# A two-layer graph attention kernel: the step whose sums are split into pieces runs for nearly all superchunks, with another order inside

## The chip, the cores and the metric

The kernel runs on one core of a Trainium2 chip. The metric is the device time of one execution in microseconds (us). The kernel before was timed three times: 4126.3, 4113.4 and 4116.05 us, median 4116.05. Besides, one execution was recorded by the hardware profiler; all durations below come from that one.

## The reference: what is computed

A graph has 6250 nodes with 256 features and 200000 directed edges with 32 features each, sorted by target node. After a layer norm and a relu, two graph attention layers follow, the first with 4 heads, the second with 1. Cut to what matters:

```python
te = relu(edge_attr @ We + be) * exp(x @ Wo + bo)[src][:, None]      # edge features
hx = (x @ Wg).reshape(n, h, f)
al = leaky_relu((hx . a_s)[src] + (hx . a_d)[dst] + ((te @ Wge) . a_e), 0.2)   # logits
m  = segment_max(al, dst);  al = exp(al - m[dst])
al = al / segment_sum(al, dst)[dst]
out = segment_sum(hx[src] * al[:, :, None], dst) + b
```

Each node also gets an edge to itself with the mean of its edges' features. The first layer's output plus its input goes through a relu into the second layer; the second layer's goes to the output. So every edge needs one row of a table indexed by its source (a gather), a softmax over all edges of one target, and a sum over all edges of one target.

## The kernel before: how the work is tiled and ordered

**Superchunks.** The edges lie in 1563 chunks of 128. A superchunk is 24 chunks; there are 66 per layer, the last two with 14 and 13 chunks. A superchunk (numbers 0 to 65 in layer 0, 66 to 131 in layer 1) takes one step of a loop (L611 to L679). The program gives the order of the instructions of each engine by hand; each engine runs its own in that order and waits by semaphores for the others.

**The work of one superchunk,** by the names in the code:

- `gather` (L872): one indirect DMA per chunk on POOL (L881) brings 128 table rows into a buffer G. There are three such buffers, so the gather of superchunk k+1 overwrites that of k-2.
- `rphase1` (L956): the edge features. For each of two halves, TensorE products into the PSUM tile y (L965), then a Relu on ScalarE (L970, or L968 for odd sizes) into R. y and R exist once. `load_ea` loads the edge features of two superchunks on SyncE.
- `spread` (L982, in every second step for two superchunks), `parts` (L1012) and `blocks` (L1027): one-hot rows and the target's share of the logits; VectorE and one small product (L1024).
- `rphase2` (L974) and `adst` (L1035): products L979 and L1038 that put edge and target shares together in the PSUM tile zad; `edge_rows` (L1041) turns them on VectorE into rt (L1052) and sums them (L1055).
- `logits` (L1058): six small VectorE operations, the first of which (L1066) is the first to read the gathered rows; the last two are running maxima.
- `ends` (L1085, product L1089), `links` (L1091: two scans L1099 and L1101 on VectorE, product L1106) and `maxima` (L1108): the maximum over each target's edges, across partitions, then the exponentials on ScalarE (L1139).
- `scale` (L1167): one VectorE operation (L1174) multiplies all rows of G by their weights.
- `carried` (L1148): adds what the superchunk before has for a target that goes on into this one.
- `onehots` (L1002, L1009): the matrix S that maps edges to target nodes.
- `sums` (L1178): per chunk one product S^T G into the PSUM tile u (L1185; each is two records in the trace). It takes the chunks a to b, so it can be called in pieces.
- `evict` (L1187) and `carry` (L1192): ScalarE copies u to U; the row to be carried on is picked by a product (L1196) and copied (L1198).
- `finish` (L1305; in layer 0 L1246 to L1275): the node window's output, on VectorE with three ScalarE operations. `rows1` and `rows2` (layer 0): transposes (L1280) and the next layer's table rows (L385). `rows3`: adds the bias (L389) with an Exp (L1292) and writes the rows to layer 1's table (L1321); in layer 1 it writes the output.

**The normal step** of superchunk k (L630 to L677) issues, in this order: the gather and the edge features of k+1, logits, ends and links of k with all 24 chunks of the sums of k-1 in one block ahead of the link product, then one-hots of k, the finish of k-2, evict and carry of k-1, maxima and scaling of k, and edge rows of k+1.

**The step in pieces** (`tight`, L710, with `meet`, L695) serves the superchunks 62 to 64 of each layer (`tight = NS - 4` at L609). There, half of the sums of k run right behind its own scaling, and the rest in the next step, in two pieces on either side of `links`. The edge features of k+1 come late in it, behind the sums, the carry and the row products of k-2 (L735). Superchunk 64, whose next one is the last, has an order of its own (`final`), which finishes two node windows.

**The end of a layer** (`last`, L751). The first 24 gathers of layer 1 are issued ahead of the last step's work. They may read only table rows that are written: the indices of `redirect` (L806) leave out the last two node windows (64 and 65), whose share is added by products afterwards (`added`, L834). So that gather needs the table write of window 63, and the gather after it those of 64 and 65.

Of the kernel before, what the change touches and what calls it, by code (L numbers as in the profile page):

```python
# [32 lines left out]
C = 24  # L33
# [45 lines left out]
class Kernel:  # L79
# [311 lines left out]
    def indices(self, wp):  # L391
# [20 lines left out]
        self.base_f = base = cp.tile([P, NS], F32, name="base")  # L412
        V.tensor_copy(base, scf[:, 0, :])
        last, qbase, qlast = scf[:, 1, :], scf[:, 3:7, :], scf[:, 7:11, :]
        yield

# [41 lines left out]
        yield  # L458
        ll = wp.tile([P, NS], F32, name="ll", bufs=1)
        V.tensor_sub(ll, last, base)  # L460
        self.lsel = cp.tile([P, NS], F32, name="lsel")
        V.tensor_scalar(self.lsel, ll, self.iota_p, None, op0=OP.is_equal)
# [109 lines left out]
    def edges(self, ctx):  # L572
        nc = self.nc
        self.gp += [self.pool(f"gath{i}", 1, ctx) for i in range(1, 3)]
        self.sp = self.pool("onehot", 2, ctx)
        self.lp = self.pool("loads", 2, ctx)
        self.wp = self.pool("work", 2, ctx)
        self.np_ = self.pool("nodes", 2, ctx)
        self.xp = self.pool("index", 1, ctx)
        self.ps_y = self.pool("ps_y", 1, ctx, space=PSUM)  # L580
        self.ps_1 = self.pool("ps_1", 1, ctx, space=PSUM)
        self.ps_f = self.pool("ps_f", 1, ctx, space=PSUM)
        self.lf = self.ps_1.tile([P, 512], F32, name="lf")
        nc.vector.memset(self.lf[0:4, 0:1], -BIG)
        offs = np.concatenate([[0], np.cumsum(self.cs)]).tolist()
        steps = [dict(L=L, s=s, C=self.cs[s], o=offs[s], k=L.l * self.NS + s)
                 for L in self.L for s in range(self.NS)]
        self.state = {0: None, 1: None}
        self.early = self.cs[0] if self.NS > 1 else 0
        self.steps = steps  # L590
        self.nodes(steps[0])
        self.load_lb(0)
        self.load_ea(0)
        self.load_fl(0)
        self.gather(steps[0], self.CX)
        if self.NS % 2:
            self.load_lb(1)
        self.spread(steps[0])
        self.parts(steps[0])
        self.blocks(steps[0])  # L600
        drain(self.rphase1(steps[0]))
        self.load_ea(1)
        self.rphase2(steps[0])
        self.adst(steps[0])
        self.edge_rows(steps[0])

        pv = pf = pr = None

        tight = max(self.NS - 4, 1)  # L609
        self.ahead, self.rest = 1, None  # L610
        for k, st in enumerate(steps):  # L611
            nx = steps[k + 1] if k + 1 < len(steps) else None
            for q in steps[k + 1:k + 3]:
                if q["L"] is st["L"] and "tw" not in q:
                    self.nodes(q)
            self.load_lb(k + 2)
            left = self.groups[self.ahead][0] - 2 - k if self.ahead < len(self.groups) else 99
            if self.rest is None and left <= 2:
                gi = self.index_load(self.ahead, self.xp)
                self.rest = self.index_group(self.ahead, self.xp, gi)  # L620
            if st["s"] + 1 == self.NS:
                self.last(st, pv, nx)
                pv = pf = pr = None
                continue
            if st["s"] >= tight:
                self.tight(st, pv, pr, nx)
                self.index_on(left)
                pr, pv = pv, st
                continue
            self.gather(nx)  # L630
            drain(self.rphase1(nx))
            self.load_ea(k + 2)
            drain(self.logits(st))
            self.ends(st)
            self.spread(nx)
            self.parts(nx)
            if pv and "u" not in pv:
                self.sums(pv)
            self.links(st)
            self.load_fl(k + 1)  # L640
            self.blocks(nx)
            if k != self.NS:
                self.onehots(st)
            if pf:
                drain(self.finish(pf))
            if pv and "U" not in pv:
                self.evict(pv)
                self.carry(pv)
            if pf:
                self.rows1(pf)  # L650
            self.rphase2(nx)
            self.adst(nx)
            drain(self.maxima(st))
            if pf:
                self.rows2(pf)
            if k == self.NS:
                self.onehots(st)
            drain(self.scale(st))
            self.carried(st)
            enter = st["s"] + 1 == tight  # L660
            if enter:
                self.sums(st, 0, self.pieces(st)[0])
            elif st["s"] == 0:
                self.sums(st)
            if pf:
                self.rows3(pf)
            self.edge_rows(nx)
            if enter:
                self.onehots(nx)
                if pv:  # L670
                    drain(self.finish(pv))
                pr = pv
            elif st["s"] == 0:
                self.evict(st)
                self.carry(st)
            self.index_on(left)
            pf, pv = pv, st  # L677
            if k == 0 and self.early:
                self.redirect()  # L679
        self.flag()  # L680
# [9 lines left out]
    def pieces(self, st):  # L690

        c = st["C"]
        return (c + 1) // 2, c - c // 3

    def meet(self, st, pv, nx):  # L695

        p1, p2 = self.pieces(pv) if pv else (0, 0)
        drain(self.logits(st))
        self.ends(st)
        if nx:  # L700
            self.spread(nx)
            self.parts(nx)
        if pv:
            self.sums(pv, p1, p2)
        self.links(st)
        if pv:
            self.sums(pv, p2)
        self.load_fl(st["k"] + 1)

    def tight(self, st, pv, pr, nx):  # L710


        final = nx["s"] + 1 == self.NS
        self.gather(nx)
        self.meet(st, pv, nx)
        self.blocks(nx)
        if final:
            self.evict(pv)
            self.carry(pv)
            if pr:  # L720
                self.rows1(pr)
                self.rows2(pr)
                self.rows3(pr)
            drain(self.finish(pv))
            drain(self.maxima(st))
            self.rows1(pv)
            self.rows2(pv)
        else:
            drain(self.maxima(st))
            self.evict(pv)  # L730
            self.carry(pv)
            if pr:
                self.rows1(pr)
                self.rows2(pr)
        drain(self.rphase1(nx))  # L735
        self.load_ea(st["k"] + 2)
        self.rphase2(nx)
        self.adst(nx)
        if final:
            self.rows3(pv)  # L740
        drain(self.scale(st))
        self.carried(st)
        self.sums(st, 0, self.pieces(st)[0])
        if pr and not final:
            self.rows3(pr)
        self.edge_rows(nx)
        self.onehots(nx)
        if not final:
            drain(self.finish(pv))

    def last(self, st, pv, nx):  # L751
# [6 lines left out]
            nc.sync.dma_start(v[:, :early * P], self.srow.partition_broadcast(P))  # L758
        if not pv:
            self.onehots(st)  # L760
        self.meet(st, pv, None)
        if nx:
            nc.vector.tensor_scalar(self.src, self.src, 2.0, None, op0=OP.mult)
        drain(self.maxima(st))
# [687 lines left out]
def drain(g):  # L1452
    for _ in g:
        pass
# [93 lines left out]
```

## Time and profile before

| what | value |
|---|---|
| median of the runs | 4116.05 us |
| the profiled execution's own time | 4109.04 us |
| span of its instructions | 4107.1 us |
| busy: POOL, VectorE, TensorE, ScalarE | 2988.5, 2872.1, 2807.1, 545.5 us |
| gathers (L881) | 3114, mean 954 ns |
| sums (L1185) | 1700.2 us busy in 6252 records |
| scaling (L1174) | 853.2 us |
| clock granted to TensorE, mean | 0.789 |
| DMA moved | 584.74 MB, 142 GB/s |

The span runs from the first to the last instruction; the profiled execution's own time lies 1.9 us above it. A group's line in the profile gives the line of code, the engine, the operation, what is written and read, the count, then the total busy time in us, the mean of one in ns, and the engine's idle time just before them with what ended it. In a timeline each row is start, duration, engine, line, operation; an idle time before it stands in brackets with its releaser. "issue" is idle time for which the profile shows no releaser.

The order of the trace: the first gather in the loop's buffers starts at 89.62 us, layer 0's last at 2057.51 us, layer 1's first at 2097.34 us and its last at 4066.99 us.

### The profile page before, as it was taken

The page shows a single profiled execution, that of the slowest core. Times are in us where ns is not written, and L with a number is a line of the kernel's source. Part 1 is how long each engine was busy: PE and PEld are TensorE (multiplying, and loading weights), DVE is VectorE, ACT ScalarE, POOL GpSimd, SP SyncE. Part 2 cuts the span into 40 slices and gives each one's busy share as a digit, 9 for nine tenths or more (in the row PEclk, how much of TensorE's full clock was granted, in tenths as well). Part 3 has the DMA queues.
Part 4 walks back from the last instruction along what each step waited for, and adds up shares of the span by engine and source line. Part 5 has one row for each costly group of instructions (what it writes and reads, how often), then busy time and mean ns, then how long its engine had stood idle before and what let it go on. Part 6 is the DMA issues. An engine that isn't in the chain of part 4 may idle for free.

```text
span 4107.1 us, 34953 instructions
## 1 busy us (share of the span) xinstructions
PE 2807.1 (68%) x10144; PEld 1848.2 (45%) x10144; DVE 2872.1 (70%) x6571; ACT 545.5 (13%) x1256; POOL 2988.5 (73%) x3158
## 2 busy tenths in 40 slices
PE   7677677776777777777676666656666566665766
PEld 5344454444444444445444444434444344443444
DVE  8677777878778787787756666566665666656566
ACT  5111111111111111111111010010100101001001
POOL 2777777777777777777647777777777777777774
PEclk9778787787787887878887777877778777777778
DMA  6555554555555555555435455555445545555543
GB/s 213 157 149 143 155 149 137 154 149 138 151 149 145 146 151 151 139 155 148 122 99 151 131 144 142 136 139 145 134 137 145 142 132 143 142 137 137 145 132 82
DMA packets 246795, 584.74 MB, mean 142 GB/s; under 512 B 63162, under 2 KB 103640, under 8 KB 246530
## 3 DMA queue, kind: packets, MB, share of 16 engines
q0 software_dynamic: 150144, 422.82, 39.4%
q1 hardware_dynamic: 96035, 158.96, 12.3%
q8 instruction: 81, 1.33, 0.1%
q14 instruction: 119, 0.97, 0.1%
q10 hardware_dynamic: 416, 0.67, 0.1%
HBM read 547.98 MB, written 34.34 MB: 142 GB/s over the span
## 4 chain that ended last, share of the span: by engine, by line
POOL 38%; PE 24%; DVE 18%; issue 15%; DMA 2%; ACT 2%; DVEq 0%; SPq 0%; ACTq 0%; POOLq 0%
POOL G L881 38%; PE u L1185 19%; DVE G L1174 8%; PE y L965 2%; DMA G<-T,src 1%; DVE lb L994 1%; PE fin L1196 1%; DVE rt L1052 1%; ACT R L970 1%; PE fin L1280 1%; ACT carry L1198 1%; DVE G L1163 1%; DVE S L1009 0%; DVE t1row L389 0%; DVE G L1143 0%
## 5 line engine op out<-in xcount | busy, mean ns | idle before, releaser
L881 POOL DMA_INDIRECT G<-T,src x3114 | 2970.2, 954 | 1075.2 <-issue 995.8
L1185 PE MATMUL u<-G,S 128*128 128x270 f32 (+1 forms) x6252 | 1700.2, 438 | 26.3 <-DVE G L1174 26.3
L1185 PEld LDWEIGHTS u<-G,S 128*128 128x128 f32 x6252 | 1354.5, 219 | 370.6 <-issue 37.8
L1174 DVE TENSOR_TENSOR G<-G,kps 128x6144 f32<-128x6144 f32 (+2 forms) x140 | 853.2, 6099 | 0.0
L965 PE MATMUL y<-ea,webd 64*128 64x384 f32 (+1 forms) x1056 | 514.1, 617 | 447.1 <-ACT R L970 442.2
L965 PEld LDWEIGHTS y<-ea,webd 64*128 64x128 f32 x1056 | 215.3, 226 | 670.2 <-ACT R L970 523.1
L1009 DVE TENSOR_TENSOR S<-kps,loc 128x3072 f32<-128x3072 f32 x132 | 436.1, 3304 | 0.0
L1089 PE MATMUL lf<-ident,fb 128*36 128x128 f32 (+1 forms) x132 | 53.4, 404 | 531.6 <-DVE fb L1081 307.5
L1089 PEld LDWEIGHTS lf<-ident,fb 128*36 128x36 f32 (+1 forms) x132 | 15.7, 119 | 647.5 <-DVE fb L1081 365.9
L970 ACT ACTIVATE R<-y,webd 128x768 f32<-128x768 f32 x260 | 231.9, 892 | 555.4 <-PE y L965 555.3
L1120 DVE SCALAR_TENSOR_TENSOR m<-fpen,lf,m 128x24 f32<-128x24 bf16 (+1 forms) x66 | 16.6, 252 | 360.2 <-PE lf L1106 359.9
L979 PE MATMUL zad<-R,wea 128*64 128x384 f32 (+1 forms) x1056 | 211.9, 515 | 0.9 <-ACT R L970 0.6
L1066 DVE TENSOR_TENSOR G<-rt,G 128x96 f32<-128x96 f32 (+1 forms) x132 | 30.1, 228 | 255.4 <-DMA G<-T,src 249.8
L1123 DVE TENSOR_TENSOR mt<-fpen,lf 128x96 f32<-128x96 bf16 (+1 forms) x66 | 16.6, 252 | 241.6 <-PE lf L1106 241.6
L1190 ACT ACTIVATE U<-u 128x270 f32<-128x270 f32 (+1 forms) x132 | 51.8, 393 | 798.4 <-PE u L1185 798.4
L1052 DVE STREAM_TRANSPOSE rt<-zad 128x768 f32<-128x768 f32 (+1 forms) x130 | 124.5, 958 | 26.7 <-PE zad L1038 26.7
L1024 PE MATMUL zad<-a,Q 128*128 128x12 bf16 (+1 forms) x132 | 23.5, 178 | 168.8 <-DVE a L1022 168.8
L1223 ACT ACTIVATE mw<-mw,mg 128x2 f32<-128x2 f32 x66 | 19.6, 298 | 863.6 <-DVE mg L1222 863.6
L994 DVE TENSOR_TENSOR lb<-lb,kps 128x1536 bf16<-128x1536 bf16 (+1 forms) x68 | 112.9, 1660 | 11.7 <-DMA lb<-locrow 11.7
L979 PEld LDWEIGHTS zad<-R,wea 128*64 128x64 f32 x1056 | 68.7, 140 | 98.4 <-issue 62.2
L1196 PE MATMUL fin<-U,lsel 128*1 128x270 f32 (+1 forms) x260 | 79.1, 385 | 41.6 <-ACT U L1190 23.2
L1099 DVE TENSOR_TENSOR_SCAN cl<-fl,cl,lf 4x129 f32<-4x129 f32 (+1 forms) x130 | 60.8, 468 | 53.2 <-PE zad L1024 52.4
(213 smaller groups left out, 2260.8 us busy)
## 6 DMA issues: line engine op xcount, KB each, us to landing
G<-T,src POOLq DMA_INDIRECT x3114, 2.8
ea<-in_ea_dram SPq DMA_DIRECT2D x64, 768.0 KB
lb<-locrow SPq DMA_DIRECT2D x64, 384.0 KB
T<-t1row SPq DMA_DIRECT2D x66, 260.0 KB
tw<-T SPq DMA_DIRECT2D x66, 258.0 KB
tw<-T SPq DMA_DIRECT2D x66, 134.0 KB
tw<-in_x_dram SPq DMA_DIRECT2D x66, 128.0 KB
out_dram<-fb SPq DMA_DIRECT2D x64, 128.0 KB
```

The lines of the kernel that those rows point to most:

```text
L881: nc.gpsimd.indirect_dma_start(out=G[:, c, 0:L.TW], out_offset=None, in_=self.rows[L.l][0:n * (1 + L.l), :], in_offset=bass.IndirectOffset ...
L965: nc.tensor.matmul(y[:, o], self.webd[l][r, :], ea[r, w], start=True, stop=True)
L970: nc.scalar.activation(R[:, i, :32 * c].rearrange("p (b n) -> p b n", b=2), y.rearrange("p (b n) -> p b n", b=2)[:, :, :16 * c], AF.Relu, ...
L979: nc.tensor.matmul(st["zad"][i * PH:(i + 1) * PH, o], self.wea[l][0], R[:, i, w], start=True, stop=False)
L994: V.tensor_tensor(lb[:, :, :n], lb[:, :, :n], self.k_part.unsqueeze(2).to_broadcast([P, i, n]), op=OP.is_equal)
L1009: nc.vector.tensor_tensor(st["S"][:, c0:c1, :], self.k_iota.unsqueeze(1).to_broadcast(w), self.loc[:, o + c0:o + c1].unsqueeze(2).to_broad ...
L1052: V.transpose(rv[:, :32 * c].rearrange("p (b n) -> p b n", b=2), z.rearrange("p (b n) -> p b n", b=2)[:, :, :16 * c])
L1089: self.nc.tensor.transpose(self.lf[0:e.shape[1], 1:P + 1], e, self.ident)
L1099: V.tensor_tensor_scan(cl[:H, :], fl[:H, :], lf[:H, 0:P + 1], init, op0=OP.add, op1=OP.max)
L1174: nc.vector.tensor_tensor(v, v, pw[:, c0:c1, :].unsqueeze(3) .to_broadcast([P, c1 - c0, H, L.F]), op=OP.mult)
L1185: nc.tensor.matmul(st["u"][:, :L.W], S[:, i, :], G[:, i, 0:L.W], start=(j == 0), stop=(j == c - 1))
L1196: nc.tensor.matmul(pr[0:1, :L.W], self.lsel[:, s:s + 1], U[:, :L.W], start=True, stop=True)
```

## The change

`tight` becomes 1: the step in pieces now serves all superchunks of a layer but its first and its last. The first enters it (`begin` and the next superchunk's one-hots at the end of its normal step).

Inside the step, the edge features of k+1 move to the front. They are issued in two halves (`next(y)`, then `drain(y)`) with a piece of the sums of k-1 between them, ahead of the logits of k. The pieces for 24 chunks are now 0 to 12 (behind the own scaling), 12 to 15, 15 to 18 and 18 to 24; before they were 0 to 12, 12 to 16 and 16 to 24. `rphase2` and `adst` now stand right behind evict, ahead of the carry; `edge_rows` stands ahead of `carried`; `rows3` behind the one-hots. In the step before `final`, `begin` issues all chunks at once, so that `final` has no sums left and evicts at its start; there `finish` of k-1 stands ahead of `rows3` of k-2, and the edge features keep their late place. `last` issues the pieces of the sums of k-1 itself; `meet` is gone.

```diff
--- before.py
+++ after.py
@@ -606,7 +606,7 @@
 
         pv = pf = pr = None
 
-        tight = max(self.NS - 4, 1)
+        tight = 1
         self.ahead, self.rest = 1, None
         for k, st in enumerate(steps):
             nx = steps[k + 1] if k + 1 < len(steps) else None
@@ -659,7 +659,7 @@
             self.carried(st)
             enter = st["s"] + 1 == tight
             if enter:
-                self.sums(st, 0, self.pieces(st)[0])
+                self.begin(st, nx)
             elif st["s"] == 0:
                 self.sums(st)
             if pf:
@@ -690,62 +690,70 @@
     def pieces(self, st):
 
         c = st["C"]
-        return (c + 1) // 2, c - c // 3
-
-    def meet(self, st, pv, nx):
-
-        p1, p2 = self.pieces(pv) if pv else (0, 0)
+        return (c + 1) // 2, (c + 1) // 2 + c // 8, (c + 1) // 2 + c // 4
+
+    def begin(self, st, nx):
+
+        self.sums(st, 0, C if nx["s"] + 2 == self.NS else self.pieces(st)[0])
+
+    def tight(self, st, pv, pr, nx):
+
+
+        final = nx["s"] + 1 == self.NS
+        p0, p1, p2 = self.pieces(pv)
+        self.gather(nx)
+        y = self.rphase1(nx)
+        if not final:
+            next(y)
+            self.sums(pv, p0, p1)
+            drain(y)
+            self.load_ea(st["k"] + 2)
         drain(self.logits(st))
         self.ends(st)
-        if nx:
-            self.spread(nx)
-            self.parts(nx)
-        if pv:
+        if final:
+            self.evict(pv)
+        self.spread(nx)
+        self.parts(nx)
+        if not final:
             self.sums(pv, p1, p2)
         self.links(st)
-        if pv:
+        if not final:
             self.sums(pv, p2)
         self.load_fl(st["k"] + 1)
-
-    def tight(self, st, pv, pr, nx):
-
-
-        final = nx["s"] + 1 == self.NS
-        self.gather(nx)
-        self.meet(st, pv, nx)
         self.blocks(nx)
         if final:
-            self.evict(pv)
             self.carry(pv)
             if pr:
                 self.rows1(pr)
                 self.rows2(pr)
+            drain(self.finish(pv))
+            if pr:
                 self.rows3(pr)
-            drain(self.finish(pv))
             drain(self.maxima(st))
             self.rows1(pv)
             self.rows2(pv)
+            drain(y)
+            self.load_ea(st["k"] + 2)
         else:
             drain(self.maxima(st))
             self.evict(pv)
+        self.rphase2(nx)
+        self.adst(nx)
+        if final:
+            self.rows3(pv)
+        else:
             self.carry(pv)
             if pr:
                 self.rows1(pr)
                 self.rows2(pr)
-        drain(self.rphase1(nx))
-        self.load_ea(st["k"] + 2)
-        self.rphase2(nx)
-        self.adst(nx)
-        if final:
-            self.rows3(pv)
         drain(self.scale(st))
+        self.edge_rows(nx)
         self.carried(st)
-        self.sums(st, 0, self.pieces(st)[0])
-        if pr and not final:
-            self.rows3(pr)
-        self.edge_rows(nx)
+        self.begin(st, nx)
         self.onehots(nx)
         if not final:
+            if pr:
+                self.rows3(pr)
             drain(self.finish(pv))
 
     def last(self, st, pv, nx):
@@ -758,7 +766,15 @@
             nc.sync.dma_start(v[:, :early * P], self.srow.partition_broadcast(P))
         if not pv:
             self.onehots(st)
-        self.meet(st, pv, None)
+        drain(self.logits(st))
+        self.ends(st)
+        if pv:
+            p0, p1, _ = self.pieces(pv)
+            self.sums(pv, p0, p1)
+        self.links(st)
+        if pv:
+            self.sums(pv, p1)
+        self.load_fl(st["k"] + 1)
         if nx:
             nc.vector.tensor_scalar(self.src, self.src, 2.0, None, op0=OP.mult)
         drain(self.maxima(st))
```

## The prediction

> **What bounds the kernel now.** I read the page's busy line first (POOL 73%, DVE 70%, PE 68%: no engine looks full), then its largest groups, then who waits for whom on POOL, then POOL's busy time by stretch, and last the timelines of the only old steps in pieces (superchunks 62 and 63) and of the turn between the layers.
>
> From the page, and from the waits of POOL over the span (total us, times, longest):
>
> ```profile
> L881 POOL DMA_INDIRECT G<-T,src x3114 | 2970.2, 954 | 1075.2 <-issue 995.8
> ```
>
> ```profile
> POOL G L881 <- issue: 995.8, 3050, 67.1
> POOL G L881 <- DVE al L1072: 38.8, 1, 38.8
> ...
> POOL G L881 <- PE u L1185: 11.1, 1, 11.1
> POOL G L881 <- DVE G L852: 7.2, 1, 7.2
> POOL G L881 <- PE lf L1106: 6.4, 9, 1.3
> ```
>
> POOL's 27% of idle time is nearly all 0.30 us between two gathers, put down to issue: once 67.1 us before the first gather, then some 929 us over 3049 gaps. A gather costs 0.95 + 0.30 = 1.25 us, so 24 of them, one superchunk, 30.1 us. The stretches say the same for each layer (us, POOL busy, gathers):
>
> ```profile
> 150.00:1950.00 1800.00, 1362.01 (x1426) 0.79 0.54 147
> 2180.00:3990.00 1810.00, 1370.77 (x1443) 0.77 0.51 139
> ```
>
> 1800/1426 = 1.262 us a gather in layer 0, 1810/1443 = 1.254 in layer 1, or 30.3 and 30.1 us a step. Layer 1's stretch has no POOL wait over 0.3 us, and there VectorE waits for gathers (L1066 behind DMA G, 246.6 us in 59 steps). In layer 0 VectorE waits 1.4 us for them in all, and POOL waits nine times for the end of a sum (6.4 us, 3.7 above the usual gap). The page's chain leads there through PE, DVE and ACT, which also need about 30.2 us. Both sides are nearly late in layer 0; POOL alone is in layer 1. **A shorter step can therefore save some 4 us in the 61 normal steps of layer 0 and nothing in those of layer 1.** What remains to win lies where POOL stands still: 11.1 + 38.8 us at the end of layer 0 and the tail after the last gather (4067.0 to 4107.1).
>
> **The old step in pieces was too long.** Logits begin at 1998.43 and 2029.87 us for superchunks 62 and 63: 31.44 us, over POOL's 30.1. The timelines show why (start, us):
>
> ```profile
> 2001.11 3.95 PE L1185 MATMUL u<-G,S 128*128 128x270 f32 x8
> 2004.99 0.32 PE L1106 MATMUL lf<-ident,cl 36*128 36x36 f32 x1
> 2005.24 3.91 PE L1185 MATMUL u<-G,S 128*128 128x270 f32 x16
> ```
>
> ```profile
> 2019.79 0.98 DVE L1052 STREAM_TRANSPOSE rt<-zad 128x768 f32<-128x768 f32 x1 [4.35 <-PE zad L1038]
> ```
>
> DVE waits 4.35 us because the edge features (L965, L979) come behind the two row products on PE. And four chunks (eight records) took 3.95 us, 494 ns a record, after PE had idled 5.51 us; the next sixteen took 244 ns each.
>
> **The new step on VectorE, row by row (layer 0).** From the end of one scaling to the next: edge rows 1.37, carry 0.98, one-hots 3.26, table row 0.34, finish 4.91 (starts 1986.70 to 1997.56), index work about 0.7 averaged, logits 1.82: 13.4 us. Then spread 1.98 in every second step, so 1.0; parts 0.84; the wait for the link transpose; maxima 2.23; scaling 6.46. In step 62 that wait ran 4.3 us from the end of parts, behind four cold chunks. Now three chunks (15 to 17) stand there: 3.3 us cold, 1.8 warm. The link scans (0.92) fit below either. Sum: 13.4 + 1.0 + 0.84 + 3.3 + 2.23 + 6.46 = 27.2 us cold, 25.7 warm. Check against the measured step: 31.44 − 4.35 (wait gone) − 1.0 (one chunk less) + 1.0 (no spread in step 62) = 27.1.
>
> **What moves, and what stands behind it.**
> - Edge features go ahead of logits. PE: twelve chunks 5.6 us (8.0 cold, as at 1986.84), first product 1.55, three chunks 1.5, second product 1.55. New wait: the first Relu (0.90) now stands on ACT behind finish's Exp and Relu, free some 10.5 us after the scaling (11.6 with index copies); the second product behind that Relu, `ends` behind the product. So `ends` is ready at 13 to 14.6 against VectorE's 13.4: 0 to 1.2 us late. Queued behind it are `parts`' product, the pieces and the link scans. Step: 25.7 to 28.4 us. Below 30.1 this costs nothing; POOL covers it, with 1.7 us left at the worse end.
> - The edge-feature load on SP (every second step) follows the second product. In the old steps that product ended about 1030.2 us and the next reader ran at 1048.93 without a wait on DMA, so 18.7 us suffice; the new order leaves about 22. Nothing.
> - Edge rows stand ahead of carry, the three carry instructions have what they need (carry's copy is done some 3 us before the scaling ends). A swap on one engine: nothing. rows3 after one-hots delays a table write by some 3 us that nobody reads in this layer.
> - Buffers: a gather needs the sums of three superchunks before, finished some 9 us into the next step, a whole step before POOL asks. The nine waits go: −3.7 us.
> - Each layer's first step keeps half its sums for later and makes one-hots (3.26) earlier. VectorE waited 1.4 us for gathers at 2172.8, so it may lag by 2 us for a step or two; POOL doesn't see it. Zero, at most 2.
> - Steps 64 and 130 (`final`) have all sums of 63 and 129 behind them. That decides the turn.
>
> **The turn.** Timeline, POOL's last gathers of 64, first of 65, last of 65, first of 66; on SP, the table write of node window 63:
>
> ```profile
> 2030.50 0.95 POOL L881 DMA_INDIRECT G<-T,src  x1 [0.30 <-issue]
> 2042.53 0.94 POOL L881 DMA_INDIRECT G<-T,src  x1 [11.09 <-PE u L1185]
> ...
> 2057.51 1.02 POOL L881 DMA_INDIRECT G<-T,src  x1 [0.30 <-issue]
> 2097.34 0.98 POOL L881 DMA_INDIRECT G<-T,src  x1 [38.81 <-DVE al L1072]
> ```
>
> ```profile
> 2091.82 0.33 SPq L1321 DMA_DIRECT2D T<-t1row  x1
> ```
>
> The waits view names an early VectorE instruction for the 38.8 us, but the gather reads layer 1's table, whose last needed rows (window 63) go out at 2091.82; 5.5 us later it starts. I take that write as the releaser. Its time in the new order: the last gather of 63 started at 2012.64, landed 2.8 later; less 3.7, logits(63) begin at about 2012 instead of 2029.87. Scaling starts 7.4 to 8.9 later and ends at 2025.7 to 2027.3. All 24 chunks then take 13.0 us on PE (48 records in 12.6 to 13.3): 2039 to 2040.5. VectorE meanwhile needs 11.5 us to logits(64) and 1.4 in them: 2038.6 to 2040.2, a tie. Evict, spread, parts and links bring finish(63) to 2041 to 2042.7; it takes 4.85. From its end to the write took 9.6 us (2082.25 to 2091.82), plus 0.35 for the table row now between: 2056 to 2057.5. **So the write is 35 us earlier, and gather 66 starts near 2062 instead of 2097.3.** Gather 65 no longer waits its 11.1 us, and POOL still idles some 17 us ahead of 66. Gather 66 (32 us), the two last table writes behind it and gather 67 (2137.33) follow unchanged, 35 us earlier; layer 1 is POOL's.
>
> **The tail.** Logits(130) began at 4058.8, with its gather landed at 4053.5. In the new order it starts near 4056; `ends` waits for the 24 chunks (4060 to 4062.5), finish(129) ends at 65 to 67 instead of 4070.7, logits(131) at 75.4 to 77 instead of 4079.85. The last step's 27.2 us stay. −3 to −4.
>
> **Sum.** −35 (−3.7 is in it) − 4 = −39: span 4107.1 → 4068; its own time 4109.0 → 4070. The median of the runs lies 7.0 above the profiled execution, so 4116.05 − 39 = **4077 us**.
>
> **A rule against the change.** The Trainium skill ("TensorE: Matmul & The Clock Gate", Part 1) says that PE falls to half its clock after about 3.4 us idle and needs as long to get back, so sums in pieces would run cold. The rows above agree in kind (494 against 244 ns after 5.51 us). PE's new gap ahead of `ends` is at most 3 us when VectorE sets the pace, some 5 when POOL does; by the rule the pieces are then cold and the step the longer of my two sums, which POOL still covers.
>
> **Rivals.**
> 1. *The pieces stay too long* (slower). If ACT's order or cold PE keeps the step at the 31.4 to 32.2 us of the old ones, layer 0 becomes a chain over 61 steps: 61 × (31.8 − 30.1) = +104, less the turn's and tail's 39, so 4180. It decides from 30.1 us a step, 1.7 to 4.4 above my sum. For it: the only measured steps in pieces. Against: 4.35 us of them are one wait that the new order removes. 11%.
> 2. *Something else holds gather 66.* If only half the 35 us come through (another write, a longer finish chain in `final`), 4085 to 4104. For it: the releaser named by the view is not my write. 13%.
> 3. *Nothing comes through at the turn*: 3.7 and 3 us remain, 4109: no difference. 6%.
> Forecast 70%.
>
> Measurements tell 0.3% (12 us, 4103.7 to 4128.4) from no change. Faster 0.83, same 0.06, slower 0.11. The likeliest case spans 4065 to 4086 (write ±2, POOL's stretched gathers ±5, runs ±3); to reach 8 in 10 the range takes in rival 2 and a little beyond the forecast's low end: 4061 to 4105.
>
> **To see afterwards.** Right: POOL still 1.25 to 1.26 us a gather; no wait on PE L1106; L1066 in layer 0 waiting 2 to 4 us a step for DMA G; the first gather of 66 at 2062, of 67 at 2102; DVE's wait on zad L1038 gone. Wrong: gathers of layer 0 waiting for PE, a layer 0 step over 30.3 us, L1089 waiting on PE's y products, or the wait ahead of gather 66 still above 30 us.

## The result, and the profile after

The changed kernel takes **4070.12 us** (median of four runs, 4067.62 to 4070.66), the kernel before, run beside it, 4119.99 us (4113.4 to 4126.3): ratio 0.9877, interval 0.9862 to 0.9893. By the medians that is 49.9 us. The profiled execution went from 4109.04 to 4070.66 us of its own time, its span from 4107.1 to 4068.9 us, 38.2 less. All that follows on where the time went is read from these two executions, so it accounts for 38.2 us; the profiled execution of the kernel before is faster than each of its four timed runs, and where the other 12 us of the medians lie, no trace shows. The clock granted to TensorE rose from a mean of 0.789 to 0.824.

From line 700 or so on, the lines of the changed kernel are 16 higher than those of the kernel before: the gather is L897, the sums L1201, the first operation of the logits L1082, the link product L1122, the table write L1337.

The two groups of the page that changed their waits, or kept them:

```profile
L897 POOL DMA_INDIRECT G<-T,src x3114 | 2968.1, 953 | 1044.2 <-issue 1002.8
...
L1082 DVE TENSOR_TENSOR G<-rt,G 128x96 f32<-128x96 f32 (+1 forms) x132 | 30.3, 229 | 664.9 <-DMA G<-T,src 663.1
```

A gather costs what it cost. VectorE now waits 663 us for gathers in all, where it waited 250 us in the kernel before, of it 1.4 us in layer 0. The stretches by layer (start and end, length, then the busy time and the number of instructions of TensorE, its weight loads, VectorE, ScalarE and POOL, then the granted clock, the DMA share and GB/s) and POOL's waits (us in total, times, longest):

```profile
150.00:1950.00 1800.00, 1329.79 (x4646) 810.08 (x4644) 1428.37 (x3351) 274.36 (x642) 1363.37 (x1428) 0.84 0.53 148
2145.00:3955.00 1810.00, 1217.61 (x4305) 776.33 (x4303) 1113.50 (x2237) 185.69 (x363) 1370.12 (x1445) 0.80 0.50 139
```

```profile
POOL G L897 <- issue: 1002.8, 3070, 67.9
POOL G L897 <- PE u L1201: 19.7, 1, 19.7
...
POOL G L897 <- PE u L865: 7.2, 1, 7.2
...
POOL G L897 <- ACT U L1206: 2.0, 1, 2.0
```

1800/1428 = 1.261 and 1810/1445 = 1.253 us a gather: both layers run at POOL's pace, as before. The nine waits behind the link product are gone, so is the 11.1 us ahead of gather 65, and the 38.8 us ahead of gather 66 are 19.7. New are 2.0 us, once, ahead of a gather of superchunk 3. At the turn of the layers, POOL's first gathers of superchunks 66 and 67, and on SyncE the table write of node window 63 with the transfer issued ahead of it:

```profile
2065.69 0.94 POOL L897 DMA_INDIRECT G<-T,src  x1 [19.70 <-PE u L1201]
...
2105.75 0.94 POOL L897 DMA_INDIRECT G<-T,src  x1 [7.16 <-PE u L865]
```

```profile
2059.35 0.40 SPq L922 DMA_DIRECT2D ea<-in_ea_dram  x1
2060.33 0.33 SPq L1337 DMA_DIRECT2D T<-t1row  x1
```

Where the 38.2 us went, from the same events in both traces:

| stretch | before | after | gain |
|---|---|---|---|
| start to the first gather of superchunk 67 | 2137.33 | 2105.75 | 31.6 |
| from there to the start of the last gather | 1929.7 | 1928.1 | 1.6 |
| end of the last gather to the end of the span | 39.2 | 34.1 | 5.1 |

Layer 0 itself gave little in these two executions: the last gather of superchunk 63 ended at 2013.6 before and at 2011.8 after. Nearly all was won in the 94 us behind it.

### The profile page after: what moved, and what is told of

It reads as the page before. It is cut to its first block, busy times and chain, and to the rows that moved or that the text cites. A ratio compares the mean times of both kernels' runs of the same rounds, so it can differ in the third digit from the quotient of the medians.

```text
span 4068.9 us, 35015 instructions
## 1 busy us (share of the span) xinstructions
PE 2858.6 (70%) x10144; PEld 1796.4 (44%) x10144; DVE 2864.2 (70%) x6571; ACT 558.8 (14%) x1256; POOL 2986.4 (73%) x3158
## 4 chain that ended last, share of the span: by engine, by line
POOL 51%; issue 19%; DVE 18%; PE 7%; DMA 4%; ACT 1%; SPq 0%; DVEq 0%; ACTq 0%; POOLq 0%
POOL G L897 51%; DVE G L1190 7%; PE u L1201 4%; DMA G<-T,src 3%; DVE S L1025 3%; DVE lb L1010 1%; DVE rt L1068 1%; PE y L981 1%; DVE m L1136 0%; DMA ea<-in_ea_dram 0%; DVE trow L389 0%; PE ps L385 0%; DVE G L1172 0%; DVE st L244 0%; PE lf L1122 0%
## 5 line engine op out<-in xcount | busy, mean ns | idle before, releaser
L897 POOL DMA_INDIRECT G<-T,src x3114 | 2968.1, 953 | 1044.2 <-issue 1002.8
L1201 PE MATMUL u<-G,S 128*128 128x270 f32 (+1 forms) x6252 | 1829.8, 450 | 177.5 <-DVE G L1190 177.2
L1201 PEld LDWEIGHTS u<-G,S 128*128 128x128 f32 x6252 | 1328.7, 220 | 630.7 <-DVE G L1190 234.4
L981 PE MATMUL y<-ea,webd 64*128 64x384 f32 (+1 forms) x1056 | 446.3, 547 | 178.8 <-ACT R L986 173.6
L1082 DVE TENSOR_TENSOR G<-rt,G 128x96 f32<-128x96 f32 (+1 forms) x132 | 30.3, 229 | 664.9 <-DMA G<-T,src 663.1
L981 PEld LDWEIGHTS y<-ea,webd 64*128 64x128 f32 x1056 | 189.0, 198 | 355.0 <-ACT R L986 202.9
L1155 ACT ACTIVATE kps<-mt 128x100 f32<-128x100 f32 (+1 forms) x132 | 29.8, 226 | 1252.8 <-DVE mt L1149 716.8
L385 PE MATMUL fin<-wg,h1T 128*128 128x260 f32 x264 | 78.4, 421 | 36.1 <-ACT h1T L1298 36.1
L1214 ACT ACTIVATE carry<-fin 1x270 f32<-1x270 f32 (+1 forms) x130 | 49.7, 382 | 260.3 <-PE fin L1212 260.3
```

What stands on the lines that cost most here:

```text
L385: self.nc.tensor.matmul(ps[:, :L.MW], hT[:, k, :], self.wg[L.l][:, k, :], start=(k == 0), stop=(k == 1))
L897: nc.gpsimd.indirect_dma_start(out=G[:, c, 0:L.TW], out_offset=None, in_=self.rows[L.l][0:n * (1 + L.l), :], in_offset=bass.IndirectOffset ...
L981: nc.tensor.matmul(y[:, o], self.webd[l][r, :], ea[r, w], start=True, stop=True)
L1201: nc.tensor.matmul(st["u"][:, :L.W], S[:, i, :], G[:, i, 0:L.W], start=(j == 0), stop=(j == c - 1))
```

## The experiments

Two runs were made on a chip where the kernel before takes 4121.68 us, as in the comparison above. Ten were made on two other chips, where it takes 4874.15 and 4916.07 us; they come last, since they answer another question.

**Theory:** in the steady state both kernels run at POOL's 30.1 us; the new order makes the step shorter than that, so the change wins only where POOL stands still, at the turn (by an earlier write of window 63, which releases gather 66) and in the tail. **Rivals:** the step is no shorter, and something else than POOL holds it; the releaser of gather 66 is another.

### How long is the new step without POOL's limit? (after20_b)

```diff
-        for c in range(c0, st["C"]):
+        n0 = 4 if 3 <= st["k"] < self.NS - 2 else c0
+        if n0 > c0:
+            nc.sync.dma_start(G[:, 0:n0, 0:L.TW], self.T[0][0:n0 * P, :].rearrange("(c p) d -> p c d", p=P))
+        for c in range(n0, st["C"]):
```

> The changed kernel with 20 gathers per superchunk of layer 0 instead of 24 (superchunks 3 to 61; the first four chunks come by one plain transfer of fixed rows, so those messages are of other rows than the reference's). Theory (the step of the new order, 26.5 to 27.5 us by itself, lies below GpSimd's 30.1 us): with 25.1 us of gathers the step of layer 0 falls to its own length, 26.5 to 27.5 us, so layer 0 loses some 59 x 3 = 177 us, and the span is near 3895 us (3880 to 3920). Rival (the step is as long as GpSimd's 30.1 us by something else): under 60 us less, 4010 us or more.

The edit reaches superchunks 3 to 63, so 61 steps have 20 gathers (2870 gathers in all instead of 3114). Measured, in one run: span 3931.2 us, own time 3933.05 us; 137.7 us less, between theory and rival, outside the theory's range and nearer to it. POOL's waits, and the stretch from 700 to 1800 us:

```profile
POOL G L900 <- issue: 907.1, 2747, 68.3
POOL G L900 <- PE u L1204: 206.6, 55, 26.4
```

```profile
700.00:1800.00 1100.00, 865.71 (x3025) 525.29 (x3024) 939.36 (x2214) 182.10 (x426) 752.69 (x788) 0.86 0.57 159
```

788 gathers are 39.4 steps of 20, so a step takes 1100/39.4 = **27.9 us**, while 20 gathers need 25.1. POOL now waits in layer 0 for the sums that free its buffer (180.0 us in 53 waits; the longest in the row above, 26.4 us, is at the turn), and VectorE waits 4.1 us in all for gathers there, where it waited 148.3: the bound has changed hands. So the step of the new order is 27.9 us long by itself, 2.2 below POOL's 30.1, and in the changed kernel POOL hides it. The expected step (26.5 to 27.5) was too short by 0.4 us or more, as the prediction's 27.2 by 0.7; 61 × (30.1 − 27.9) = 134 of the 138 us.

### Does the write of window 63 release gather 66? (write_early_b)

```diff
             self.rows2(pv)
+            self.rows3(pv)
             drain(y)
...
         self.adst(nx)
-        if final:
-            self.rows3(pv)
-        else:
+        if not final:
             self.carry(pv)
```

> The changed kernel with one edit: in the last step of layer 0 the two row sums and the table row of superchunk 62 (rows3, with the transfer of the rows) stand ahead of the second y product of that step instead of behind it, so the table's pieces can leave earlier. Theory (at the turn of the layers the first gather of superchunk 66 waits for the table write of superchunk 63, and nothing else of the turn is later): the write starts 2 to 5 us before 2060.3 us of the changed kernel's span, the first gather of superchunk 66 as much before 2065.7, and the span is 4064 us against 4068.9. Rival (the write of superchunk 63 waits for ScalarE's work of finish(63), which the edit does not touch): the span is within 1 us of 4068.9. On the chip of the first eight runs this kernel took 5414 us against 4874 of the kernel before; if that comes of the chip, this run on another chip is near 4065; if it comes of the kernel, the ratio of about 1.11 comes again.

The text above names superchunk 62 and the last step; the edit moves the row of window 63, in the step of superchunk 64, ahead of both products of the edge features. Measured: 4067.66 us median (4063.04 to 4070.95, four runs), ratio to the kernel before 0.9861, interval 0.9835 to 0.9888. The profiled execution's span was 4069.1 us: as the rival said. But its turn went as the theory said. SyncE's two table writes (one row; the second, of window 63, starts 0.33 us before its end, at 2057.07) and the transfer that followed, then POOL:

```profile
2052.39 5.01 SPq L1336 DMA_DIRECT2D T<-t1row  x2
2060.65 0.40 SPq L921 DMA_DIRECT2D ea<-in_ea_dram  x1
```

```profile
2059.89 0.95 POOL L896 DMA_INDIRECT G<-T,src  x1 [13.10 <-DMA T<-t1row]
```

The write is 3.3 us earlier and the gather 5.8, and now the trace names the write itself as releaser. **That settles the releaser.** The 2.5 us more come from the queue: in the changed kernel the edge features' transfer was issued 0.98 us ahead of the write and its packets began first, at 2060.4; the write's packets ran from 2062.9 to 2064.5, through 4.2 us after the write was issued. Here the write goes first and its packets are through at 2058.7, 1.7 us after it.

Gather 67 was 6.0 us earlier, too (2099.78). Where did that go? 3.8 us went up to the last gather, 3.5 of them in the 1539 gathers' mean of 951.3 ns instead of 949.0, which nothing in the edit explains and which is within what runs differ. The rest, 2.4 us, is missing from the last gather to the end (36.5 us instead of 34.1). It was lost on TensorE, in the one block of sums of superchunk 129; in the changed kernel and here:

```profile
4016.78 10.83 PE L1201 MATMUL u<-G,S 128*128 128x261 f32 x48 [1.99 <-DVE G L1190]
```

```profile
4014.36 13.52 PE L1200 MATMUL u<-G,S 128*128 128x261 f32 x48 [3.35 <-DVE G L1189]
```

The same 48 records took 13.52 instead of 10.83 us, after an idle time of 3.35 instead of 1.99 us; the granted clock from 4014 to 4028 us was 0.79 instead of 1.00. It stood at 0.50 from 4013.0 to 4019.9, so for the block's first 5.5 us, which at half the clock is the 2.7 us lost. Begun 2.4 us earlier, the sums ended 0.3 later, and so began the product of `ends` for superchunk 130, which stands behind them (4027.72 instead of 4027.44). The Trainium skill ("TensorE: Matmul & The Clock Gate", Part 1) states a busy or idle window of about 3.4 us that runs freely, so that the moment of the switch varies. The pair of rows agrees in kind; but the clock fell 2.0 us after the last product before the gap (4011.0), so less than 3.4 us of idling was enough here. By the median this version is 0.16% under the changed kernel, which its interval does not tell from nothing.

### Ten runs on two other chips

On these chips, the kernel before takes 4874.15 (the first) and 4916.07 us (the second) instead of 4120, and every run there is slow (15 of it on the first: 4863.52 to 4887.0). Whether the chip itself or something around it makes the difference, no run tells; below, "these chips" means no more. The edits that were not yet shown:

```diff
 last4, last12, last12_b (changed kernel)
-        tight = 1
+        tight = max(self.NS - 4, 1)        # 12 for last12 and last12_b
 early_start3 (the edit of write_early_b, and)
+        tight = 3
 old_pieces_all (kernel before)
-        tight = max(self.NS - 4, 1)
+        tight = 1
 features_late, features_late_b (changed kernel)
-            next(y)
             self.sums(pv, p0, p1)
-            drain(y)
-            self.load_ea(st["k"] + 2)
         drain(self.logits(st))
...
-        self.rphase2(nx)
-        self.adst(nx)
-        if final:
-            self.rows3(pv)
-        else:
+        if not final:
             self.carry(pv)
...
+            drain(y)
+            self.load_ea(st["k"] + 2)
+        self.rphase2(nx)
+        self.adst(nx)
+        if final:
+            self.rows3(pv)
```

write_early has the edit of write_early_b, after20 and before20 that of after20_b (before20 in the kernel before).

> The new step in pieces, but only for the superchunks that had the old one (62 to 64 of each layer); all others keep the normal step. Theory (POOL sets the pace of the steady steps; the gain is made at the turn between the layers and in the tail): entering late costs VectorE some 13 us of lag, of which the new step (27 to 28 us against POOL's 30.1) has one or two steps to win back. Logits of 63 begin near 2026, the table write of window 63 near 2072, gather 66 near 2078 instead of 2097.3: 19 us of the 32 are there, and 5 of the tail. Span 4083, own time 4085, ratio to before 0.994. Rival (the gain is spread over all the steady steps, 38/132 = 0.3 us each): nearly nothing is left, 4105 to 4107.

> As the kernel after, but the step in pieces serves only the superchunks 54 to 64 of each layer. Theory: some 2.6 us are won back per step, so after five or six steps logits wait for the gather, and the turn and the tail are those of the kernel after; layer 0's normal steps keep most of their waits for sums (about 3 us), and the 2.05 us wait of gather 3 at the start is gone. Span 4070 to 4072, ratio to before 0.990 to 0.991: within 0.1% of the kernel after. Rival (gain spread over all steps): 11 of 64 steps, 4107 - 7 = 4100.

> The changed kernel with the new step for the last 10 full steps of layer 0 only (from superchunk NS-12 on; the steps before that as in the kernel before). Theory (in the steady state both steps take GpSimd's 30.1 us, and the gain is made at the turn of the layers, by how soon superchunk 63 is finished): nearly all of the gain stays, span 4069 to 4082 us against 4068.9 of the changed kernel and 4107.1 of the kernel before, ratio to the kernel before 0.988 to 0.991. Rival (the gain is gathered over all 60 steps): a sixth of it stays, span near 4101 us, ratio 0.998.

> The kernel after, and in the step of superchunk 64 the table row of window 63 (its Exp on ScalarE and its write) goes ahead of the next edge features instead of behind them. Theory (that write releases gather 66): the Exp no longer stands behind two Relus (2055.1 to 2060.0), the write goes out 4.5 us earlier, gather 66 and all of layer 1 too: 4068.9 - 4.5 = 4064.4 span. Rival (something else releases gather 66, as the releaser named by the waits suggests): no change, 4068.9.

> As the one with the early write, and the step in pieces begins at each layer's fourth superchunk instead of the second. Theory: the wait of gather 3 for the sums of superchunk 0 (2.05 us, 1.75 over the usual gap) came from halving these sums while VectorE was still 20 us behind; it goes and no other takes its place: 4062.6 span. Rival: the wait moves on to gather 5 (4064.4).

> The kernel after, but in layer 0's superchunks 3 to 63 only 20 of the 24 chunks are gathered on POOL; four come by one plain load of fixed rows from SyncE, so the rows are not the edges' own. This measures the new step without POOL's bound: POOL needs 20 x 1.254 = 25.1 us a step. Theory: VectorE's chain then sets the pace, 27.2 us (25.7 to 28.4), logits no longer wait, layer 0 is 60 x 2.9 = 175 us shorter (100 to 260): span near 3895. Rival (the chain is really as long as the old pieces' 31.4 us and was hidden): no change, 4069. Rival (POOL sets the pace even so): 60 x 5.0 = 300 shorter, 3770.

> The kernel before with the same four chunks per superchunk of layer 0 (3 to 63) by a plain load of fixed rows. Theory: the normal step has its own chain of PE, VectorE and ScalarE just under POOL's 30.1 us; without POOL's bound it takes 29 to 30.2, so only 0 to 70 us are saved: span 4040 to 4107. The difference to the kernel after with 20 gathers then is what the change did to the step, some 2.5 us, which the full kernel can't use. Rival (the old step was only waiting on POOL): 27 us or less, 180 us saved.

> The kernel before with the step in pieces for all superchunks but each layer's first, its inner order unchanged. Theory: the old order needs 31.4 us, 32.2 with spread and index work; layer 0 becomes a chain over 61 steps of 1.3 to 2.1 us above POOL: 80 to 130 us more, less the 13 us that before lost on entering: span 4170 to 4225. Layer 1 (27.6 us) is unchanged. Rival (pieces everywhere are the gain, the order is not): 4070.

> The kernel after with one part undone: the edge features of the next superchunk go back behind the carry and the row products. Theory: VectorE's wait ahead of the edge rows comes back, 4.4 to 4.6 us a step in layer 0, the step is 31.6 to 31.8 us: 61 x 1.6 = 100 us more, and some 15 at the turn, where logits of 63 come late: span 4170 to 4185. Rival (the sizes of the pieces or the sums themselves made the difference): 4069 to 4080.

> The changed kernel with the new step's order undone: the edge features' products are back behind the sums as in the step that the kernel before took for its last two superchunks, and the sums stay in pieces for all superchunks but the first. Theory (the order brings the step below GpSimd's 30.1 us: 27.9 us measured with 20 gathers against some 31.4 us of the old step in pieces): GpSimd waits 1 to 2 us in each step of layer 0, span 4130 to 4190 us, slower than the kernel before. Rival (pieces alone are enough, the order is not needed): span 4065 to 4080 us.

Measured (steps of layer 0 from the logits of superchunk 10 to those of 60, of layer 1 from 76 to 126; POOL's waits over 0.6 us, per step of the former stretch; all in us):

| run | time, us | ratio to before | step, layer 0 | step, layer 1 | POOL waits |
|---|---|---|---|---|---|
| last4 | 4873.71 | 0.9995 [0.9981, 1.0008] | 36.6 | 34.3 | 6.7 |
| last12 | 4940.28 | 1.0139 [1.0115, 1.0163] | 37.2 | 35.1 | 7.2 |
| last12_b (second chip) | 4981.03 | 1.0131 [1.0112, 1.0149] | 37.4 | 35.5 | 7.4 |
| write_early | 5414.04 | 1.1116 [1.1092, 1.1140] | 40.5 | 39.2 | 10.6 |
| early_start3 | 5416.43 | 1.1112 [1.1089, 1.1135] | 40.6 | 39.4 | 10.8 |
| features_late | 5647.58 | one run | 42.7 | 41.0 | 13.1 |
| features_late_b (second chip) | 5686.93 | one run | 43.3 | 41.0 | 13.6 |
| old_pieces_all | 5691.58 | one run | 43.6 | 40.8 | 13.9 |
| after20 | 5193.74 | one run | 37.1 | 39.5 | 12.3 |
| before20 | 4582.24 | one run | 31.7 | 34.3 | 6.9 |

Every expectation in microseconds failed here, since each had POOL's 30.1 us as the bound, and here it bounds nothing: a step of 36 to 44 us contains the same 30.1 us of gathers (25.1 in after20 and before20) and a wait. **The change is a loss on these chips, as far as write_early stands for it:** the changed kernel itself was not run there; write_early, which differs from it by one call in one step of each layer, is 11% slower than the kernel before, and as write_early_b 1.4% faster than it on a chip of the first kind. The more of a layer's steps are the new one (the last few in last4, some ten in last12, nearly all in write_early), the slower.

The same program on both kinds of chip shows what differs. From who waits for whom, write_early on the first other chip and write_early_b:

```profile
ACT R L985 <- remote: 1640.6, 140, 33.7
POOL G L896 <- PE u L1200: 1252.0, 118, 48.4
...
DVE cl L1114 <- remote: 832.1, 60, 21.2
```

```profile
ACT R L985 <- PE y L980: 466.6, 198, 26.7
...
DVE cl L1114 <- PE zad L1039: 15.4, 9, 5.3
```

POOL, which waits for the sums 118 times in the first, does not wait for them in the second; the Relu and the first link scan wait 1640.6 and 832.1 us there for an event without a name, and 466.6 and 15.4 us for their products on the other. It is not the work: a gather is 0.955 us in both, the scaling 6.10, a packet of a gather 174 and 172 ns, one of SyncE's queue 84 and 82. Idle time of VectorE behind 150 us is 2472 instead of 1161 us, of POOL 2319 instead of 990, of TensorE 2312 instead of 1169. Where it lies, a timeline of VectorE in write_early shows; POOL had begun a row of 24 gathers at 979.88 us and its last ended at 1009.97:

```profile
995.46 0.41 DVE L1287 TENSOR_TENSOR t1row<-tw,hw 128x256 f32<-128x256 f32 x1
...
996.51 0.25 DVE L532 CAST gf<-gi 128x192 f32<-128x192 int32 x1
998.21 0.26 DVE L537 TENSOR_TENSOR gt<-gf,base 128x96 f32<-128x96 f32 x1 [1.44 <-DVE gf L532]
...
1001.71 0.21 DVE L547 TENSOR_SCALAR fpen<-gt 128x96 bf16<-128x96 f32 x1 [2.42 <-issue]
...
1003.81 0.21 DVE L547 TENSOR_SCALAR lpen<-gt 128x96 bf16<-128x96 f32 x1 [1.72 <-remote]
...
1006.61 0.32 DVE L1083 TENSOR_TENSOR al<-G 128x96 f32<-128x96 f32 x1 [2.16 <-issue]
1008.70 0.32 DVE L1085 TENSOR_TENSOR al<-al,ade 128x96 f32<-128x96 f32 x1 [1.77 <-remote]
1010.10 0.26 DVE L1087 SCALAR_TENSOR_TENSOR al<-al 128x96 f32<-128x96 f32 x1 [1.08 <-DVE al L1085]
1010.80 0.36 DVE L1094 TENSOR_TENSOR_SCAN fb<-pen,al 128x96 f32<-128x96 bf16 x1 [0.44 <-DVE al L1087]
```

Up to 996.51 us, about the fourteenth gather of this row, most small operations follow each other at 0.1 to 0.45 us. Then many come 1.4 to 2.7 us after the one before, mostly with nothing that the profile can name to hold them, and soon after the last gather the old rhythm is back. Over 55 steps of layer 0, VectorE's idle time put down to "issue" or "remote" is 0.1 us a step in the first 12 us of a row of gathers (some ten of them), 8.3 us in the next 24 and none behind that; in write_early_b it is 0.01 us a step in all. SyncE shows the same in its bookkeeping: of its 661 register instructions (MOVE and FUSED_REGOPS), 158 take 0.6 us or more in this trace, 258 and 257 in last12 and last12_b, and none in write_early_b, where half of them take 0.04 us or less and the longest 0.18. The releaser "remote" is the profile's word for an event it cannot place; there is only one core here.

So the time between instructions that depend on each other is what is longer on these chips, and every step there is bound by that chain. That more hand-overs within a step (sums in pieces wait for the scaling, the links, the Relus) cost more there is a likely reason for the loss, and the steps of the table go that way; the hand-overs were not counted, nor separated from where in the step they lie, so this is not shown. Why instructions start so late there beside a row of gathers, and why only from about the tenth on, stays open.

Two things carry over. The order does shorten a step in pieces: features_late to write_early −2.2 us and old_pieces_all to write_early −3.1 us a step in layer 0, both on the first of these chips, against the 4.35 us wait that the prediction saw it remove. And fewer gathers shorten the step there, too (36.6 in last4 to 31.7 in before20, 40.5 in write_early to 37.1 in after20, pairs that differ besides only in steps near a layer's end), although POOL waits in it: slow stretches end with the row of gathers, which fits, and is no proof. Two things stay open: whether the last ten steps alone bring the whole gain on a chip of the first kind (last12), and what the old order in pieces would cost there. That layer 0 gave 1.8 us is said by the events of two traces, not by a run.

## Why the prediction was right

- **POOL's pace as the bound.** 1.261 and 1.253 us a gather after, 1.262 and 1.254 before. Right, and after20_b shows it by taking four gathers away.
- **The new step, 27.2 us (25.7 to 28.4).** 27.9 us measured, on the long side. The terms are in the changed kernel's timeline of TensorE, one step of layer 0:

```profile
1008.95 1.55 PE L981 MATMUL y<-ea,webd 64*128 64x384 f32 x4
1010.43 1.63 PE L1201 MATMUL u<-G,S 128*128 128x270 f32 x6
1015.96 2.92 PE L981 MATMUL y<-ea,webd 64*128 64x384 f32 x4 [3.89 <-ACT R L986]
...
1022.00 3.05 PE L1201 MATMUL u<-G,S 128*128 128x270 f32 x6
```

  The second product waits 3.89 us for the Relu behind finish's work on ScalarE, as foreseen, and then runs cold, that is at half the granted clock (0.50): 2.92 us; the sum had 1.55. The three chunks ahead of the links are cold as well (0.52), 3.05 us against 3.3 in the cold sum. The other pieces of the step are not: three chunks in 1.63 us ahead of the product, six behind the links in 3.00, both at 1.00. So the rule against the change holds for one piece, and POOL covers it; its 3.4 us were not needed here either, since the clock fell 2.6 us after the product before the gap had ended (1012.1 to 1014.7).
- **What is late next.** VectorE waits for gathers in layer 0: 148.3 us in 44 waits from 150 to 1950 us, 2.5 us a step over 60 steps; 2 to 4 were predicted. No wait on the link product is left on POOL.
- **The turn, −35.** It gave 31.6. Event by event:

| event | predicted | measured |
|---|---|---|
| logits of 63 begin | 2012 | 2013.71 |
| its scaling ends | 2025.7 to 2027.3 | 2029.2 |
| its sums end (24 chunks) | 2039 to 2040.5 | 2040.5 |
| finish of 63 begins | 2041 to 2042.7 | 2044.75 |
| write of window 63 | 2056 to 2057.5 | 2060.33 |
| gather 66 | 2062 | 2065.69 |

  Two terms were mis-sized. The nine waits of 3.7 us went, but 2.0 us came at superchunk 3 (the entry into the new step, priced at "Zero, at most 2"), so gathers of 63 ended 1.8 us earlier, not 3.7. That wait is not there in write_early_b, whose code is the same up to superchunk 64, and there the gathers of 63 ended at 2012.55, later than here (2011.80), so these 2 us are of the size by which executions differ. And finish(63) waits 1.07 us for a ScalarE operation behind the copy of the transposes, which the sum had at nothing. Two more errors cancelled, which is luck: the index work ahead of logits(64), averaged at 0.7 us a step, lay just here, 2038.15 to 2040.9, but the one-hots and the edge rows for a superchunk of 14 chunks are shorter, so VectorE needed 11.7 us to logits(64) against 11.5. The sums took 11.2 us and not 13. From finish's end the sum holds: 9.8 us to the write against 9.6 + 0.35, and 5.4 to the gather against 5.5.
- **The tail, −3 to −4.** It gave 5.1: logits(130) began 2.8 us nearer to the last gather, as predicted, logits(131) 5.1 nearer where 2.9 to 4.5 was. The last step took 27.3 us, the 27.2 of before.
- **Layer 1, nothing.** 1.6 us: gathers of 949.0 instead of 950.0 ns on average.
- **The sum.** −39 predicted, −38.2 measured between the traces; an own time of 4070 predicted, 4070.66 measured. That it is so near is in part luck: the turn came 3.4 us short, the tail and layer 1 gave 2.7 to 3.7 more than forecast. The 7 us between 4070 and the 4077 on record are the distance of the first three runs' median from the profiled execution, carried over. That term had nothing behind it but three runs, and it did not carry over: the changed kernel's median lies 0.5 us below its profiled execution, while that of the kernel before, with its fourth run, lies 11.0 above. So the medians differ by 49.9 us where 39 was forecast (39 us less than 4119.99 is a ratio of 0.9905, outside the interval of 0.9862 to 0.9893), and the account above explains 38.2 of them.
- **The rivals.** The pieces stay too long: false here, and true on the two other chips by another cause than the one given: the added time there lies between instructions. Something else holds gather 66: false, by write_early_b. Nothing comes through: false.

## What to carry to other kernels

When one engine's queue sets the pace of a loop, a shorter step wins next to nothing inside the loop (1.8 of 38.2 us here came from layer 0's steps, by the traces); look for where that engine stands still, and follow back from there what it waits for, with the transfers that stand ahead in the same queue (2.5 us here). A chain moved up by 6 us can give 2.4 of them back further on through a TensorE at half its clock, so compare the whole span, not the place of the edit. A step that is hidden by 2 us under one engine's pace is hidden only while hand-overs cost what they do: on another chip of the same type the same order with one call moved (write_early) was 11% slower, so a tuning that adds hand-overs should be timed on more than one chip.

## What the runs showed of the hardware

On two of the chips used here the same programs took 18 to 33% longer (4874 against 4120 us, 5414 against 4068 us) with the same durations of gathers (0.955 us), scaling (6.10 us) and packets (174 and 172 ns). The loss is time between instructions, on VectorE, ScalarE, TensorE and SyncE but not between two gathers on GpSimd (0.30 us in both), from about the tenth gather of each row on: 8.3 us a step on VectorE in write_early, where write_early_b has 0.01.

Twice the granted clock fell from 1.00 to 0.50 less than 3 us after TensorE's last product: 2.6 us in the changed kernel (1014.7) and 2.0 us in write_early_b (4013.0).
